# A graph layer on one core: a void block and the odd group at the front, one set of node windows at the end, and a catch-up of five for four

## The chip, the cores and the metric

One core of one Trainium2 chip. The metric is device microseconds for one execution, the median of several runs (three for the kernel before: 2513.2 us, 2512.73 to 2515.78). The engines are PE (TensorE: matmuls and their weight loads), DVE (VectorE), ACT (ScalarE), POOL (GpSimd, which here mostly issues gathers) and SP (which here only issues transfers). They run beside each other, each through its own list of instructions in order, and wait for one another by semaphores.

## What is computed

A graph network layer with a layer norm ahead of it: 6250 nodes of 256 numbers, 206250 edges sorted by destination, 33 per node on average, 64 attributes and one polarity per edge.

```python
h = jnp.maximum(_layernorm(x, axis=-1), 0.0)
polarity = jnp.clip(edge_attr[:, 0:1], 0.0, 1.0)
e = jax.nn.relu(raw @ W_e1.T + b_e1) @ W_e2.T + b_e2
edge_emb = (e * (polarity + 0.01)) @ W_le.T + b_le
msg = jax.nn.relu(h[src] + edge_emb)
aggr = jax.ops.segment_sum(msg, dst, num_segments=h.shape[0])
g = (h + aggr) @ W_g1.T + b_g1
hn = (g - mu) * jax.lax.rsqrt(var + LN_EPS) * ln_g + ln_b
out = x + jax.nn.relu(hn) @ W_g2.T + b_g2
```

All in float32.

## The kernel before

Units, blocks, groups. A tile is 128 edges. A block is four tiles (512 edges), a group is six blocks (GE = 3072 edges). 67 full groups and one odd block of 426 edges make NB = 403 blocks. A unit is half a block, two tiles; there are 806 units. A pair is two blocks that share one load of raw attributes (`load_pair`, L234). In a group the tiles are laid out so that each of the four tiles of a block covers its own run of destinations; `sel` (L589) is a matrix of 128 edges by 32 rows that says which edge adds to which row.

Per pair, `first_layer` (L239) does the first edge layer: eight records of L250 on PE, each block giving two 128x512 results in PSUM that ACT (L259, three of them) and DVE (L256, one) pass through a relu into `e1`. Per unit, `edge_part` (L266) multiplies by the product of the two following weight matrices (four matmuls, eight records, L274) and DVE adds a bias into `msg` (L279); where `plain(u)` holds, in a third of the first units, ACT copies instead (L277) and DVE adds the bias later (L607). `turn_of` (L291) is called at every fourth unit and puts in the next layers, the sums that have become possible and the next loads; in the middle of the run it does two pairs at a time every eighth unit. PSUM has seven banks in one ring for all this (`psz`, L226) and one for the sums.

The other half of a unit is `whole` (L601): DVE multiplies the message by the polarity and adds the gathered row of `hb_d` (L609, two instructions), ACT applies the relu (L614). `hb_d` is the normalized input plus b_le; POOL gathers its rows (L560). The first four units (RAW) are gathered straight from x before `hb_d` exists (L347); their statistics (L457 to L462), normalization (L466) and b_le (L605) are done apart. `add_up` (L616) sums whole units into a group's rows in PSUM (L626), `keep` (L633) copies a finished group to `ms`.

The lead-in (L432 to L459) goes through x in 13 chunks, twelve of four tiles and one of 106 rows: DVE takes statistics (`stats`, L369), ACT a square root (`root`, L376), ACT and POOL make the rows, SP stores them (`nodes_out`, L380). Between the chunks it puts LEAD = 22 units of the edge work. Their `whole` halves must wait for `hb_d`; the main loop (L779 to L801) catches up on them, two whole units for each new one, until they stand a fixed lag behind. That lag is 18 units at first and one at the end.

Nodes are finished in 49 windows of 128 (`node_work`, L674) as soon as the groups that reach into them are summed: `rows_of` (L720) adds the groups' rows to the node (L726), `one`, `two` and `three` are the first matmul (L170) with statistics, the transposition (L186) and the second matmul (L196) with the addition of x (L198) and the store. They are put between units by a list of due units. Two windows are left for the end, since their last group is the last full one or the odd block: window 47 and window 48. Their steps are written out by hand in L802 to L830. In `windows_of` (L64) a group reaches MARGIN = 768 edges beyond its own; a check on the real destinations (`verdict`, L526) sends inputs that exceed this to another way through the data (`any_order`).

The order on each engine is the order in which the program issues the work (`tc.manual_schedule()`).

## Time and profile before

| | us |
|---|---|
| runs of before | 2512.73, 2513.20, 2515.78 (median 2513.2) |
| profiled execution | 2537.35 |
| its span, first to last instruction | 2535.6 |
| mean granted clock of PE in it | 0.967 of full speed |
| busy in the span: PE / DVE / POOL / ACT | 2368.3 / 1657.0 / 1634.3 / 983.4 |
| lead-in and catch-up, as shown below | 0 to 135 |
| from the last edge matmul to the last addition | 2515.46 to 2530.20 |

In the profile, a row of a group has the line, engine, operation, what it writes from what it reads, shapes and count, then busy time and mean duration in ns, then the idle time of the engine just before and who ended it. A row of the timeline has its start, its length, engine, line and operation, the count of instructions merged into it, and in brackets the idle time before it with the one that ended it. "issue" is time in which the engine waited for nothing that the profile shows. Busy time of PE is modelled and instructions overlap, so that starts to starts say more than durations. A float32 matmul shows as two records.

### The profile page before, as it was taken

To read this page: it belongs to the slowest core of one execution; us is meant where nothing else is said; L and a number is where in the kernel's file an instruction comes from. 1 tells how busy PE (TensorE), PEld (TensorE's weight loads), DVE (VectorE), ACT (ScalarE), POOL (GpSimd) and SP (SyncE) were. 2 spreads that over 40 slices of the span, in tenths; PEclk is the share of its full clock that TensorE was granted. 3 is DMA by queue.
4 is the path that set the end of the run, shared out by engine and by line. 5 is a ranking of instruction groups with operands and counts; after the bars stand their busy time and mean duration, and the time that the engine had idled before them with its cause. 6 is when DMAs were issued, how large, how long until landed. Compare 5 with 4: busy or idle time off the path is not lost.

```text
span 2535.6 us, 35656 instructions
## 1 busy us (share of the span) xinstructions
PE 2368.3 (93%) x12382; PEld 1669.2 (66%) x12382; DVE 1657.0 (65%) x3975; ACT 983.4 (39%) x1710; POOL 1634.3 (64%) x1675
## 2 busy tenths in 40 slices
PE   9989999999999999999999999999999999999978
PEld 6666666676766666666766766666766666666646
DVE  7866566666767666665666666666766666666736
ACT  7433333333433433343333333333433333333313
POOL 7666666666666666666666666666666666666661
PEclk9999999999999999999999999999999999999979
DMA  9444344433443443434343444344334334433441
GB/s 308 132 119 121 105 126 119 125 119 106 120 134 115 126 119 102 132 112 127 120 129 112 127 117 120 107 123 121 117 115 128 118 113 118 126 115 109 121 117 41
DMA packets 156226, 309.23 MB, mean 122 GB/s; under 512 B 33327, under 2 KB 78088, under 8 KB 156040
## 3 DMA queue, kind: packets, MB, share of 16 engines
q0 software_dynamic: 77376, 211.39, 28.8%
q1 hardware_dynamic: 77364, 92.23, 11.6%
q10 hardware_dynamic: 1300, 3.28, 0.4%
q8 instruction: 98, 1.61, 0.3%
q14 instruction: 88, 0.72, 0.1%
HBM read 293.92 MB, written 12.85 MB: 121 GB/s over the span
## 4 chain that ended last, share of the span: by engine, by line
PE 86%; issue 6%; DVE 5%; another core or an unknown queue 1%; ACT 1%; DVEq 0%; ACTq 0%
PE pz L274 53%; PE pz L250 17%; PE pd L626 10%; PE pz L726 2%; PE pz L170 2%; PE pz L196 2%; DVE hg L609 2%; DVE msg L279 1%; ACT e L259 1%; PE pz L186 1%; DVE st L141 0%; DVE e L256 0%; DVE sel L589 0%; ACT xt L388 0%
## 5 line engine op out<-in xcount | busy, mean ns | idle before, releaser
L560 POOL DMA_INDIRECT hg<-hb_d,src_s x1604 | 1589.3, 991 | 842.5 <-issue 481.3
L274 PE MATMUL pz<-wc_s,e 128*128 128x256 f32 x6448 | 1484.4, 385 | 34.3 <-issue 26.7
L274 PEld LDWEIGHTS pz<-wc_s,e 128*128 128x128 f32 x6448 | 1220.1, 192 | 303.9 <-issue 95.2
L614 ACT ACTIVATE hg<-hg 128x512 f32<-128x512 f32 x805 | 507.1, 631 | 934.3 <-DVE hg L609 760.2
L279 DVE TENSOR_TENSOR msg<-pz,bc_s 128x512 f32<-128x512 f32 x799 | 547.1, 686 | 233.7 <-remote 86.8
L609 DVE SCALAR_TENSOR_TENSOR hg<-msg,pol_s,hg 128x256 f32<-128x256 f32 x1612 | 697.0, 480 | 0.4
L256 DVE TENSOR_SCALAR e<-pz,vecs 128x512 f32<-128x512 f32 x201 | 150.4, 748 | 568.7 <-PE pz L250 192.3
L250 PE MATMUL pz<-raw,we_s 64*128 64x512 f32 x1612 | 480.2, 661 | 24.3 <-issue 18.3
L259 ACT ACTIVATE e<-pz,vecs 128x512 f32<-128x512 f32 x605 | 376.3, 685 | 318.0 <-remote 112.9
L626 PE MATMUL pd<-hg,sel 128*32 128x256 f32 x3216 | 280.5, 389 | 82.8 <-issue 74.6
L250 PEld LDWEIGHTS pz<-raw,we_s 64*128 64x128 f32 x1612 | 170.5, 198 | 240.9 <-issue 176.4
L626 PEld LDWEIGHTS pd<-hg,sel 128*32 128x32 f32 x3216 | 116.0, 110 | 264.2 <-issue 215.0
L589 DVE SCALAR_TENSOR_TENSOR sel<-iota_w,zero_c,rel 128x128 f32<-128x128 f32 x403 | 138.6, 344 | 0.0
L638 ACT ACTIVATE ms<-pd 128x256 f32<-128x256 f32 x66 | 25.3, 384 | 257.9 <-PE pz L274 92.8
L726 PE MATMUL pz<-s,ms 128*128 128x128 f32 x548 | 74.6, 280 | 6.1 <-issue 5.6
L726 PEld LDWEIGHTS pz<-s,ms 128*128 128x128 f32 x548 | 71.1, 194 | 11.6 <-issue 7.7
L701 DVE SCALAR_TENSOR_TENSOR hT<-hT,zero_c,stb 128x128 f32<-128x128 f32 (+1 forms) x196 | 67.1, 343 | 2.3 <-issue 2.3
L170 PE MATMUL pz<-wg_s,hT 128*128 128x256 f32 (+1 forms) x196 | 51.6, 386 | 7.0 <-DVE hT L728 4.7
L196 PE MATMUL pz<-wg_s,nT 128*128 128x256 f32 (+1 forms) x196 | 51.2, 381 | 1.3 <-issue 0.6
L170 PEld LDWEIGHTS pz<-wg_s,hT 128*128 128x128 f32 (+1 forms) x196 | 36.1, 190 | 16.1 <-DVE hT L728 7.5
L196 PEld LDWEIGHTS pz<-wg_s,nT 128*128 128x128 f32 (+1 forms) x196 | 37.0, 190 | 7.7 <-issue 1.7
L392 POOL TENSOR_TENSOR hb<-xt,rows_b 128x256 f32<-128x256 f32 (+1 forms) x49 | 34.2, 729 | 12.0 <-issue 5.4
(98 smaller groups left out, 415.4 us busy)
## 6 DMA issues: line engine op xcount, KB each, us to landing
raw<-in_raw_t_dram SPq DMA_DIRECT2D x202, 256.0 KB
hg<-hb_d,src_s POOLq DMA_INDIRECT x1604
stb<-st_d SPq DMA_DIRECT2D x49, 128.0 KB
hb_d<-hb SPq DMA_DIRECT2D x12, 512.0 KB
xt<-in_x_dram SPq DMA_DIRECT2D x48, 128.0 KB
hT<-in_x_t_dram SPq DMA_DIRECT2D x48, 128.0 KB
out_dram<-ot SPq DMA_DIRECT2D x48, 128.0 KB
xt<-in_x_dram SPq DMA_DIRECT2D x11, 512.0 KB
```

What stands on the lines that cost most here:

```text
L196: nc.tensor.matmul(po[:n, 0, :], nT[:, c, :n], wg2_s[:, c, :], start=c == 0, stop=c == 1)
L250: z = nc.tensor.matmul(pe[s, c], we1_s[s * F:(s + 1) * F, c * P:(c + 1) * P], raw[q][s * F:(s + 1) * F, :], start=True, stop=True)
L256: nc.vector.tensor_scalar(e1[b][:, c, :], pe[s, c], be1_s[:, c:c + 1], 0.0, op0=ALU.add, op1=ALU.max)
L259: nc.scalar.activation(e1[b][:, c, :], pe[s, c], AF.Relu, bias=be1_s[:, c:c + 1])
L274: last_z = nc.tensor.matmul(pz[:, i, :], e1[b][:, c, k:k + P], wc_s[:, c, :], start=c == 0, stop=c == 1)
L279: nc.vector.tensor_add(msg[u], pz, bc_s)
L560: g = nc.gpsimd.indirect_dma_start(out=hg[u][:, i, :], out_offset=None, in_=hb_d, in_offset=bass.IndirectOffsetOnAxis(ap=src_s[:, 2 * u + ...
L589: nc.vector.scalar_tensor_tensor(sel[g][:, k * S:(k + 1) * S, :], iota_w.rearrange("p (o w) -> p o w", o=1).to_broadcast([P, S, W]), zero_ ...
L609: nc.vector.scalar_tensor_tensor(hg[u][:, i, :], m[:, i, :], pol_s[:, 2 * u + i:2 * u + i + 1], hg[u][:, i, :], op0=ALU.mult, op1=ALU.add)
L614: nc.scalar.activation(hg[u], hg[u], AF.Relu)
L626: z = nc.tensor.matmul(acc[g][j * W:(j + 1) * W, :], sel[g][:, k * S + j, :], m[:, j % 2, :], start=k == 0, stop=b == blocks_of(g)[-1])
L726: nc.tensor.matmul(pa[:, c, :n], ms[g][:, c * P:(c + 1) * P], box["sel2"][i][:, :n], start=i == 0, stop=i == len(gs) - 1)
```

## The change

The odd group moves to the front: block 0 is void and never computed, block 1 is group 0 (512 edges), groups 1 to 67 are full and the last one carries the padding. There are still 403 blocks with work and 806 units, now numbered 2 to 807 (U0 = 2). The first raw tile has one block in it, so the first layer has half its matmuls; the first call of `turn_of` comes at unit 2. All that ran at a unit's number in the main loop is shifted by U0, except the turns, which stay on multiples of four and eight.

In the catch-up five whole units are made for every four new ones instead of two for one. In the lead-in the last full chunk of x and the chunk of 106 rows are both stored one step earlier, with the statistics of the short one ahead; the statistics of the four raw units take their scratch from pool `w0` instead of `p1`. At the end only window 48 is left, because the last group reaches back by LAST = 512 edges; its sums of the earlier group and the bias of its first matmul are put ahead of the last whole units, the last group is copied in halves by ACT and DVE, and what is due of other windows comes between its steps. `dst` and the check on destinations follow the new layout.

```diff
@@ -31,11 +31,14 @@
 NF = E // GE
-NB = NF * L + 1
+NB = NF * L + 2
 NT = NB * S
...
 MARGIN = 768
+SP = S * P
+LAST = 512
+U0 = 2
 DEG = E // N
...
@@ -54,17 +57,18 @@
 def group_of(b):
-    return b // L
+    return (b + L - 2) // L
 
...
 def blocks_of(g):
-    return range(g * L, min((g + 1) * L, NB))
+    return range(max(1, 2 + (g - 1) * L), 2 + g * L)
 
...
 
-    lo = (GE * g - MARGIN) // DEG
-    hi = (GE * (g + 1) + MARGIN) // DEG
+    a, b = (SP + GE * (g - 1), SP + GE * g)
+    lo = (a - (LAST if g == NG - 1 else MARGIN)) // DEG
+    hi = (b + MARGIN) // DEG
     return [w for w in range(NW) if w * P <= hi and (w + 1) * P > lo]
...
@@ -162,14 +166,17 @@
 
-        def first(aT, bias_by_pe=False):
+        def bias():
             ph = ps()
-            if bias_by_pe:
-                nc.tensor.matmul(ph[:n, 0, :], ones[0:1, :n], bg1_b[0:1], start=True, stop=False)
+            nc.tensor.matmul(ph[:n, 0, :], ones[0:1, :n], bg1_b[0:1], start=True, stop=False)
+            return ph
+
+        def first(aT, begun=None):
+            ph = ps() if begun is None else begun
             for c in range(2):
-                nc.tensor.matmul(ph[:n, 0, :], aT[:, c, :n], wg1_s[:, c, :], start=c == 0 and not bias_by_pe, stop=c == 1)
+                nc.tensor.matmul(ph[:n, 0, :], aT[:, c, :n], wg1_s[:, c, :], start=c == 0 and begun is None, stop=c == 1)
             hs = nd.tile([P, D], F32, name="hs")
-            if bias_by_pe:
+            if begun is not None:
                 hb = ph[:, 0, :]
...
@@ -177,7 +184,8 @@
             one_over_std(rs[:n], mv, n)
-            nc.vector.tensor_scalar(hs[:n], hb[:n], mv[:n, 0, 0:1], rs[:n], op0=ALU.subtract, op1=ALU.mult)
+            for h in ([slice(0, P), slice(P, D)] if begun is not None else [slice(0, D)]):
+                nc.vector.tensor_scalar(hs[:n, h], hb[:n, h], mv[:n, 0, 0:1], rs[:n], op0=ALU.subtract, op1=ALU.mult)
             return hs
...
@@ -238,20 +246,20 @@
 
-            bs = [b for b in (2 * q, 2 * q + 1) if b < NB]
+            bs = [b for b in (2 * q, 2 * q + 1) if 1 <= b < NB]
             if not bs:
...
             for c in range(2):
-                for s, b in enumerate(bs):
+                for s, b in ((b % 2, b) for b in bs):
                     pe[s, c] = ps().rearrange("p a b -> p (a b)")
...
             for c in range(2):
-                for s, b in enumerate(bs):
+                for s, b in ((b % 2, b) for b in bs):
                     if s == c == 1:
...
@@ -261,7 +269,7 @@
 
-            return u < LEAD and u % 3 == 1
+            return u < U0 + LEAD and u % 3 == 1
 
...
@@ -306,7 +314,7 @@
             edge_part(u)
-            if u % 4 == TURN:
+            if u % 4 == TURN or u == U0:
                 turn_of(u // 4)
...
@@ -326,7 +334,7 @@
-        nc.scalar.dma_start(out=src_0, in_=src_c[:, :2 * RAW])
+        nc.scalar.dma_start(out=src_0, in_=src_c[:, 2 * U0:2 * U0 + 2 * RAW])
...
@@ -430,17 +437,23 @@
             for k in range(len(parts) + 1):
-                if k < len(parts):
+                last = len(parts) - 1
+                if k < last - 1:
                     stats(k, 0, 2)
+                if k == last:
+                    stats(k, 0, CH)
+                    root(k)
                 if k == 0:
...
                     product()
-                if k:
+                if 0 < k <= last:
                     nodes_out(k - 1)
                     load_rows(k - 1 + AHEAD)
-                if k < len(parts):
-                    stats(k, 2, CH)
+                if k == last:
+                    nodes_out(k)
+                if k < last:
+                    stats(k, 2 if k < last - 1 else 0, CH)
                     root(k)
...
@@ -455,7 +468,7 @@
                 for m in range(n * RAW // 2, (n + 1) * RAW // 2):
-                    row_stats(p1, P, 2, lambda i: hg[m][:, i, :], mv_0[:, 2 * m:2 * m + 2, :])
+                    row_stats(w0, P, 2, lambda i: hg[U0 + m][:, i, :], mv_0[:, 2 * m:2 * m + 2, :])
                 forward(u)
...
@@ -479,17 +492,17 @@
-            nc.tensor.matmul(pb[:, :NF, :], ones[0:1, :],
-                             dst_f[0:1, :full].rearrange("o (g r) -> o g r", r=L * S)[:, :, :S], start=True, stop=True)
-            nc.tensor.matmul(pb[:, NF, :], ones[0:1, :], dst_f[0:1, full:], start=True, stop=True)
+            nc.tensor.matmul(pb[:, 1:, :], ones[0:1, :],
+                             dst_f[0:1, 2 * S:].rearrange("o (g r) -> o g r", r=L * S)[:, :, :S], start=True, stop=True)
+            nc.tensor.matmul(pb[:, 0, :], ones[0:1, :], dst_f[0:1, S:2 * S], start=True, stop=True)
...
-                rel[:, :full].rearrange("p (g k j) -> p g k j", k=L, j=S),
-                dst_f[:, :full].rearrange("p (g k j) -> p g k j", k=L, j=S),
-                base_b[:, :NF, :].rearrange("p g (o j) -> p g o j", o=1).to_broadcast([P, NF, L, S]), ALU.subtract)
-            nc.vector.tensor_tensor(rel[:, full:], dst_f[:, full:], base_b[:, NF, :], ALU.subtract)
+                rel[:, 2 * S:].rearrange("p (g k j) -> p g k j", k=L, j=S),
+                dst_f[:, 2 * S:].rearrange("p (g k j) -> p g k j", k=L, j=S),
+                base_b[:, 1:, :].rearrange("p g (o j) -> p g o j", o=1).to_broadcast([P, NF, L, S]), ALU.subtract)
+            nc.vector.tensor_tensor(rel[:, S:2 * S], dst_f[:, S:2 * S], base_b[:, 0, :], ALU.subtract)
...
@@ -573,7 +587,7 @@
                 spent += us
-                while (got - 2 * RAW) * STEP < spent + AFLOAT and got < 2 * min(NU, 4 * summed + HG):
+                while (got - 2 * (U0 + RAW)) * STEP < spent + AFLOAT and got < 2 * min(NU, max(U0, 4 * summed) + HG):
                     gather(behind)
...
@@ -583,7 +597,7 @@
 
-                t = (g * L + k) * S
+                t = blocks_of(g)[k] * S
                 if k == 0:
...
@@ -616,9 +630,9 @@
-                k = b - g * L
+                k = b - blocks_of(g)[0]
...
-                    acc[g] = pd[:, g % 2, :] if g < NG - 1 else ps()[:, 0, :]
+                    acc[g] = pd[:, g % 2, :]
...
@@ -634,10 +648,12 @@
                     ms[g] = ms_p.tile([P, D], F32, name="ms")
-                    if g != NG - 2:
-                        nc.scalar.activation(ms[g], acc.pop(g), AF.Copy)
+                    a = acc.pop(g)
+                    if g < NG - 1:
+                        nc.scalar.activation(ms[g], a, AF.Copy)
                     else:
-                        nc.vector.tensor_copy(ms[g], acc.pop(g))
+                        nc.scalar.activation(ms[g][:, :P], a[:, :P], AF.Copy)
+                        nc.vector.tensor_copy(ms[g][:, P:], a[:, P:])
                     sel.pop(g)
...
@@ -651,9 +667,9 @@
                     for b in (2 * summed, 2 * summed + 1):
-                        if b < NB:
+                        if 1 <= b < NB:
                             whole_groups.append(add_up(b))
-                            if b % L == 0 and group_of(b) + 2 < NG:
+                            if b == blocks_of(group_of(b))[0] and group_of(b) + 2 < NG:
                                 rest.extend(select(group_of(b) + 2))
...
@@ -710,6 +726,10 @@
 
+                def begin():
+                    sums_of(gs[:-1])
+                    box["ph"] = bias()
+
                 def halves_out():
...
@@ -727,17 +747,17 @@
                                                    op1=ALU.add)
-                    if gs[-1] < NG - 2:
+                    if gs[-1] < NG - 1:
                         at(now + far_apart[0], one)
...
                 def one():
-                    box["hs"] = first(box["hT"], gs[-1] >= NG - 2)
-                    if gs[-1] < NG - 2:
+                    box["hs"] = first(box["hT"], box.get("ph"))
+                    if gs[-1] < NG - 1:
                         at(now + far_apart[1], two)
...
                     box["nT"] = second(box["hs"])
-                    if gs[-1] < NG - 2:
+                    if gs[-1] < NG - 1:
                         at(now + far_apart[2], three)
...
@@ -747,9 +767,9 @@
                     at(now + 2, spread)
-                if gs[-1] < NG - 2:
-                    return lambda: at(now + 2, rows_of)
-                ending[gs[-1] - NG].append((sums_of, halves_out, rows_of, one, two, three, gs))
+                if gs[-1] < NG - 1:
+                    return lambda: at(now + 2 - (gs[-1] == NG - 2), rows_of)
+                ending.append((begin, sums_of, halves_out, one, two, three, gs))
                 return lambda: None
...
@@ -771,12 +791,12 @@
                           (8, node_weights)):
-                at(LEAD + i, fn)
+                at(U0 + LEAD + i, fn)
             for i, fn in enumerate((by_group(0, ALU.max), by_group(1, ALU.min), by_row(0, ALU.max), by_row(1, ALU.min),
                                     verdict, count, total)):
-                at(LEAD + 22 + 5 * i, fn)
+                at(U0 + LEAD + 22 + 5 * i, fn)
             flag = None
-            for u in range(LEAD, NU):
+            for u in range(U0 + LEAD, NU):
                 now = u
...
@@ -784,8 +804,8 @@
                 piece()
-                lag = max(LEAST, LEAD - RAW - u // SHRINK) + (by_two(u // 4) and (u + 1) % 8 == TURN)
-                ready_for = min(u + 1 - lag, 2 * (u + 1 - LEAD))
+                lag = max(LEAST, LEAD - RAW - (u - U0) // SHRINK) + (by_two(u // 4) and (u + 1) % 8 == TURN)
+                ready_for = min(u + 1 - lag, U0 + 5 * (u + 1 - U0 - LEAD) // 4)
                 while made < ready_for:
...
@@ -797,35 +817,25 @@
                             late[w] = node_work(w, True)
-                if u == LEAD + 60:
+                if u == U0 + LEAD + 60:
                     flag = nc.values_load(bad_i[0:1, 0:1], min_val=0, max_val=3 * P)
+            while steps:
+                steps.popleft()[1]()
+            for begin, sums_of, halves_out, one, two, three, gs in ending:
+                begin()
+            while made < NU:
+                whole(made)
+                made += 1
+            add_pairs(last=True)
+            for begin, sums_of, halves_out, one, two, three, gs in ending:
+                sums_of(gs[-1:])
+                halves_out()
+                one()
             while todo:
...
                     fn()
-            while steps:
-                steps.popleft()[1]()
-            before, last = ending[-2], ending[-1]
-            for sums_of, halves_out, rows_of, one, two, three, gs in before:
-                rows_of()
-            for sums_of, halves_out, rows_of, one, two, three, gs in last:
-                sums_of(gs[:-1])
-            while made < NU:
-                whole(made)
-                made += 1
-            for sums_of, halves_out, rows_of, one, two, three, gs in before:
-                one()
-            add_pairs(last=True)
-            for sums_of, halves_out, rows_of, one, two, three, gs in last:
-                sums_of(gs[-1:])
-                halves_out()
-            for sums_of, halves_out, rows_of, one, two, three, gs in before:
-                two()
-            for sums_of, halves_out, rows_of, one, two, three, gs in last:
-                one()
-            for sums_of, halves_out, rows_of, one, two, three, gs in before:
-                three()
-            for sums_of, halves_out, rows_of, one, two, three, gs in last:
+            for begin, sums_of, halves_out, one, two, three, gs in ending:
                 two()
...
@@ -954,12 +964,11 @@
 
-        a = padded(a, NT * P, fill)
-        a = a.reshape((NT, P) + a.shape[1:])
-        o = np.empty_like(a)
-        n = NF * L * S
-        o[:n] = np.swapaxes(a[:n].reshape((NF, S, L) + a.shape[1:]), 1, 2).reshape(o[:n].shape)
-        o[n:] = a[n:]
+        a = padded(a, (NT - S) * P, fill)
+        a = a.reshape((NT - S, P) + a.shape[1:])
+        o = np.full((NT, P) + a.shape[2:], fill, a.dtype)
+        o[S:2 * S] = a[:S]
+        o[2 * S:] = np.swapaxes(a[S:].reshape((NF, S, L) + a.shape[1:]), 1, 2).reshape(o[2 * S:].shape)
         return o
```

36 lines of the change are left out of this document (18 added, 18 removed).

## The prediction

> **What bounds the kernel now.** I read the page first (shares, the chain of waits, the costliest groups), then windows of a few microseconds, then the timeline of the first 135 us and of the last 30.
>
> ```profile
> PE 2368.3 (93%) x12382; PEld 1669.2 (66%) x12382; DVE 1657.0 (65%) x3975; ACT 983.4 (39%) x1710; POOL 1634.3 (64%) x1675
> ...
> PE 86%; issue 6%; DVE 5%; another core or an unknown queue 1%; ACT 1%; DVEq 0%; ACTq 0%
> ...
> L274 PE MATMUL pz<-wc_s,e 128*128 128x256 f32 x6448 | 1484.4, 385 | 34.3 <-issue 26.7
> ...
> L614 ACT ACTIVATE hg<-hg 128x512 f32<-128x512 f32 x805 | 507.1, 631 | 934.3 <-DVE hg L609 760.2
> ...
> L250 PE MATMUL pz<-raw,we_s 64*128 64x512 f32 x1612 | 480.2, 661 | 24.3 <-issue 18.3
> ...
> L626 PE MATMUL pd<-hg,sel 128*32 128x256 f32 x3216 | 280.5, 389 | 82.8 <-issue 74.6
> ```
>
> PE (TensorE) carries 86% of the chain. Nearly all of that is per unit of edges (L274), per pair of blocks (L250) and per summed block (L626), and the change leaves those counts alone: 806 units and 403 blocks before and after (the void block has no matmul). So only the places where PE waits can pay: the start, where VectorE (DVE) is behind, and the end.
>
> ```profile
> 76.93:80.74 3.81, 0.00 (x1) 0.03 (x1) 3.77 (x8) 1.26 (x2) 3.23 (x2) 1.00 0.23 70
> 82.60:89.90 7.30, 6.80 (x17) 3.26 (x15) 6.17 (x15) 5.35 (x9) 5.19 (x5) 0.55 0.35 97
> 2440.00:2470.00 30.00, 15.87 (x34) 8.98 (x34) 0.61 (x2) 1.66 (x4) 19.35 (x21) 0.51 0.33 95
> ```
>
> In these windows the columns are length, busy time of PE, its weight load, DVE, ACT, POOL, granted clock, DMA share and GB/s. PE stands still for 3.81 us while DVE is busy for 3.77, and then runs 7.3 us at 0.55 of its clock. The last row is a stretch in which PE crawls with nobody to wait for. It explains most of why the profiled execution (2537.35 us, span 2535.6, so 1.75 around it) is 24.2 us over the median 2513.2. I work out differences in the profiled execution and apply them to the median; this stretch is no part of the edit.
>
> **The change part by part: the lead-in.** The order of the changed kernel's instructions shows PE doing one unit, not two, ahead of the layer of the third raw tile.
>
> ```profile
> 14.14 3.62 PE L274 MATMUL pz<-wc_s,e 128*128 128x256 f32 x16
> 18.69 1.99 PE L250 MATMUL pz<-raw,we_s 64*128 64x512 f32 x8 [0.93 <-DMA raw<-in_raw_t_dram]
> ...
> 17.58 0.69 DVE L279 TENSOR_TENSOR msg<-pz,bc_s 128x512 f32<-128x512 f32 x1 [1.95 <-ACT xt L388]
> ...
> 21.00 0.72 DVE L256 TENSOR_SCALAR e<-pz,vecs 128x512 f32<-128x512 f32 x1
> ```
>
> That layer waits for its DMA until 18.69, and the loads ahead of it on SP's queue are the same. So the second unit falls behind it. Unit cost: 64 records of L274 take 14.01 us (row below), eight units, 1.75 each. DVE gets the layer's fourth relu straight after the first message, so it sits from about 18.2 to 20.65 in front of five statistics blocks that used to fill that time; 2.4 us late there; how much of that is made up before 65 I leave to the bounds. I take PE's 1.75; bounds 0 and 2.8 (the whole of 15.9 to 18.69). The first unit of the main loop then starts at 66.88 + 1.75 = 68.6 (66.88 is the end of the L250 that begins below at 64.96 and takes 1.92).
>
> ```profile
> 60.50 0.42 DVE L141 BATCH_NORM_STATS2 st<-hg 128x6 f32<-128x256 f32 x1
> ...
> 61.05 0.40 DVE L141 BATCH_NORM_STATS2 st<-hg 128x6 f32<-128x256 f32 x1
> ...
> 64.96 1.99 PE L250 MATMUL pz<-raw,we_s 64*128 64x512 f32 x8
> ...
> 66.93 0.98 POOL L560 DMA_INDIRECT hg<-hb_d,src_s  x1 [3.34 <-DVE msg L279]
> ...
> 68.57 0.99 DVE L468 TENSOR_SCALAR pol_s<-pol_s 128x1612 f32<-128x1612 f32 x1
> 68.69 4.04 ACT L466 ACTIVATE hg<-hg,nm,rs 128x256 f32<-128x256 f32 x8 [0.47 <-DVE nm L462]
> ...
> 71.83 0.88 DVE L609 SCALAR_TENSOR_TENSOR hg<-msg,pol_s,hg 128x256 f32<-128x256 f32 x2
> 72.62 0.69 DVE L605 TENSOR_TENSOR hg<-hg,rows_b 128x512 f32<-128x512 f32 x1
> 73.23 0.69 DVE L607 TENSOR_TENSOR msg<-msg,bc_s 128x512 f32<-128x512 f32 x1
> 73.95 0.88 DVE L609 SCALAR_TENSOR_TENSOR hg<-msg,pol_s,hg 128x256 f32<-128x256 f32 x2
> ...
> 78.38 1.83 DVE L488 TENSOR_TENSOR rel<-dst_f,base_b 128x1608 f32<-128x1608 f32 x1
> 80.51 0.69 DVE L279 TENSOR_TENSOR msg<-pz,bc_s 128x512 f32<-128x512 f32 x1
> 81.11 0.34 DVE L589 SCALAR_TENSOR_TENSOR sel<-iota_w,zero_c,rel 128x128 f32<-128x128 f32 x1
> 81.38 0.68 DVE L607 TENSOR_TENSOR msg<-msg,bc_s 128x512 f32<-128x512 f32 x1
> 94.24 1.13 DVE L506 TENSOR_SCALAR rowid<-base_b,p 32x68 f32<-32x68 f32 x4
> ```
>
> Starts to starts give DVE's prices: message 0.60, whole unit 0.79, b_le 0.61, the bc addition 0.71, sel 0.27, rel 1.87 (with its short second half), polarity twice 0.99, row numbers 1.15, one statistics block 0.55 (60.50 to 61.05, two instructions), relu of a layer at most 0.72.
>
> **The catch-up.** Before, DVE makes two whole units for each unit of PE from the first, and the first sums stand at the fourth; PE waits for their sel (3.81), then for messages. In the changed kernel the eight statistics blocks of the raw rows come after the relu of the layer at 65.1 (68.6 less two units), one sum step of five blocks comes at unit 33 instead of one of two and one of four, and units 24 and 25 are followed by two layers at once. DVE's list from 65.1 to the whole of unit 11, which the last of those sums needs: 3 relus 2.1, statistics 4.4, the root of their variances 0.4 (an estimate, two short operations), polarity 2.0, 9 messages 5.4, 10 wholes 7.9, 4 b_le 2.4, 3 bc 2.1, rel 1.9, 5 sel 1.35, row numbers 1.15: 31.1, ending at 96.2; with ACT's relu (631 ns in its group) that is 96.8.
>
> PE meanwhile: two units to 72.1, four layer matmuls to 74.0. The next four need banks: the third of them the message of unit 25 (75.8 in DVE's list) and the fourth ACT's first relu, which stands behind eight normalizations (4.04 us from 70.7) and the relu of a whole unit, so until 76.5. PE resumes with unit 26 at about 77.1. Eight units 14.0 and the small matmuls 0.7 end at 91.8, a layer at 93.7, three of the five blocks' sums at 95.2; the rest waits to 96.8 and ends at 97.3. The next layer waits for the message of unit 33 (98.8: two messages, a whole and two sel after 96.2) and ends at 99.8. Eight units, layer, four blocks, layer (14.0 + 1.92 + 2.0 + 1.92) bring unit 42 to 119.6. DVE's list in that time is 19 us, so it no longer decides.
>
> ```profile
> 109.09 14.01 PE pz L274 x64
> 123.10 1.92 PE pz L250 x8
> ...
> 135.09 4.95 PE pz L274 x22
> ```
>
> Before, unit 42 starts at 135.09. There 764 units are left, in the changed kernel 766, half a layer more (0.96) and one block's sum (0.5): 3.5 + 1.0 + 0.5 = 5.0. From 123.10 to 135.09 the rows of before hold 12.0 us for work worth 1.92 + 2.0 + 1.92; the other 6.1 are issue waits after a burst of small matmuls, which I charge to both. The head gains 135.09 - 6.1 - 119.6 - 5.0 = 4.4. Lower bound: the catch-up saves nothing and the lead-in's 2.8 stay (-2.8); upper bound: the 6.1 go too (+10.5).
>
> By the rows, each wait of PE in that sketch is under 2 us. With a dip of the clock like the one above it would lose 7.3 x 0.45 = 3.3. [...]
>
> Edits at nothing: the scratch from another pool and the order of the last two chunks let the first gather go earlier, which stood 3.34 us for DVE at 66.93. No PE work waits for it: whole units read gathered rows only from the fifth on, about 81 in my list. If that cover is gone it is worth at most those 3.34, not counted.
>
> **The end.**
>
> ```profile
> 2515.39 1.93 PE L626 MATMUL pd<-hg,sel 128*32 128x256 f32 x32
> 2515.50 0.69 DVE L279 TENSOR_TENSOR msg<-pz,bc_s 128x512 f32<-128x512 f32 x1
> 2517.25 1.92 PE L726 MATMUL pz<-s,ms 128*128 128x128 f32 x12
> ...
> 2520.60 1.13 PE L170 MATMUL pz<-wg_s,hT 128*128 128x256 f32 x4
> 2521.66 0.64 PE L626 MATMUL pz<-hg,sel 128*32 128x256 f32 x8
> ...
> 2523.07 0.69 PE L710 MATMUL pz<-s,ms 128*128 128x106 f32 x4 [0.77 <-ACT ms L638]
> 2523.58 0.49 DVE L717 SCALAR_TENSOR_TENSOR hT<-hT,pz 128x106 f32<-128x106 f32 x2
> 2525.77 0.43 DVE L141 BATCH_NORM_STATS2 st<-pz 106x6 f32<-106x256 f32 x1 [1.70 <-PE pz L170]
> 2529.78 0.42 DVE L198 TENSOR_TENSOR ot<-pz,xt 106x256 f32<-106x256 f32 x1 [1.93 <-PE pz L196]
> ```
>
> From PE's last edge unit (2515.46) to the end of the last addition (2530.20) are 14.74. In the changed kernel the chain is: 0.3 of DVE backlog, the message 0.60, two wholes 1.58 and their relu 0.6 (3.1); last sums 0.25 and half a copy each on ACT and DVE 0.35 (3.7, estimates); L710's two matmuls and the two halves 1.0 (4.7); the second half of L170 0.6 (5.3); from the statistics to the end 4.43 as before, less 0.1 for the split (9.6). That saves 5.1. But window 47's work moves ahead of that point, onto a busy PE: 12 records of L726 (1.7, the 1.92 of the row less the short wait for ms inside it), L170 1.07, and three blocks' sums, 24 of the 32 records in 2.0 (1.5): 4.3. Net 0.8; bounds -1.5 (a DVE backlog of a whole unit and message more, and window 47's matmuls late) and +3 (part of the 4.3 falls into waits PE has anyway).
>
> Sum: 4.4 + 0.8 = 5.2 us off; 2537.35 would be 2532.1, and the median 2508.0.
>
> **The rivals.**
>
> 1. Little is left: a half clock returns once (-3.3) and the end brings nothing (-0.8), so 1.1 remain: 2512.1. For it: DVE is busy at every moment from 65 to 98 in my list, so any slip reaches PE. Against: PE needs only the last two of five blocks' sums late.
>
> 2. Slower. Mechanism: DVE does not clear its backlog, because the statistics (4.4) now stand behind the relu at 65.1. Then PE waits at the sums of units 33, 41 and 49, each wait long enough for a half clock. Price: 2 us and 3.3 each, three times, 16, against a head of 4.4 and an end of 0.8: 10.7 over, and 5.4 over with two of the three; 2518.6 to 2523.9. It decides from the point where unit 11's whole is later than about 101, four us past my list. For it: the row 76.93 shows this very wait. Against: DVE's share over the span is 65%, and the 19 us list between units 34 and 42 fits.
>
> 3. The issue waits after the first bursts (6.1) go with the smaller backlog: 2508.0 - 6.1 = 2501.9. For it: they follow the burst in which DVE had just caught up. Against: 74.6 us of issue idle before L626's matmuls in the whole run.
>
> **How the numbers follow.** Forecast 0.48, rival 1 0.25, rival 2 0.15, rival 3 0.12. About 0.2% (5.0 us) is what a measurement of this kernel can tell from no change. The forecast lies just beyond it, and its own range, 2502 to 2512 from the smaller unknowns, lies more on the faster side than not, since the upper bounds of both terms are wider than the lower; I count 0.36 of its chance as faster and 0.12 as same. Rival 1 is the same, rival 3 faster, rival 2 slower but for 0.02. Faster 0.36 + 0.12 = 0.48, same 0.12 + 0.25 + 0.02 = 0.39, slower 0.13. The range reaches down to 2500 for rival 3 and up to 2518.5 for the start of rival 2.
>
> **What would show it.** Unit 2 done by 16 and the next L274 only after 20.6; DVE in front of a relu at 18 to 20. No PE pause over 3 us between 66 and 120, and no 0.5 clock there; a short PE wait at sums near 95. Unit 42 between 119 and 126. At the end one set of statistics, about 9.6 us from the last edge matmul to the last addition. Wrong, if PE pauses over 3 us again before its sums, if DVE is still full after 125, or if the end is longer than 12.

## The result and the profile after

Side by side on one chip, 22 runs each, the changed kernel took 2521.97 us (median; 2513.17 to 2530.76) and the kernel before 2514.57: ratio 1.0025, interval 1.0013 to 1.0036. By the ratio that is 6.3 us slower (the two medians stand 7.4 apart), where 5.2 faster was forecast. In the later sets the kernel before took 2181 us in two and 2554 to 2557 in three, one chip giving both at different hours, so only ratios inside a set are compared. The unchanged text of the changed kernel, over all sets:

```
set of runs          before, us   ratio changed / before   interval
first                2514.6       1.0025                   1.0013 to 1.0036
a2_changed_again     2180.6       0.9998                   0.9989 to 1.0007
a3_changed_third     2556.7       1.0000                   0.9975 to 1.0024
a4_changed_fourth    2555.0       1.0007                   0.9990 to 1.0024
a5_changed_fifth     2555.0       0.9973                   0.9956 to 0.9990
```

The last two are the same text beside the same runs of before and stand 0.34% apart, so the intervals are too narrow for what one kernel does from one load to the next. The first set's 0.25% was not seen again; the five ratios average 1.0001. What has to be explained is less a loss than why neither term of the forecast gain arrived.

The page of the changed kernel (first profile, 2529.66 us, span 2527.9), engines and the chain:

```profile
PE 2364.1 (94%) x12376; PEld 1666.4 (66%) x12376; DVE 1655.9 (66%) x3978; ACT 983.0 (39%) x1710; POOL 1636.8 (65%) x1675
...
PE 85%; issue 6%; DVE 5%; another core or an unknown queue 2%; DMA 1%; ACT 1%; SPq 0%; DVEq 0%; ACTq 0%
```

Nearly the shares of before, with DMA new in the chain. Its timeline of PE, and three windows of it (columns as in the prediction):

```profile
13.86 1.89 PE L282 MATMUL pz<-wc_s,e 128*128 128x256 f32 x8
20.07 3.78 PE L258 MATMUL pz<-raw,we_s 64*128 64x512 f32 x8 [4.32 <-DMA raw<-in_raw_t_dram]
...
75.48 3.70 PE L258 MATMUL pz<-raw,we_s 64*128 64x512 f32 x12
80.20 2.69 PE L258 MATMUL pz<-raw,we_s 64*128 64x512 f32 x4 [1.01 <-DVE msg L287]
82.82 3.78 PE L282 MATMUL pz<-wc_s,e 128*128 128x256 f32 x8
...
102.00 1.98 PE L258 MATMUL pz<-raw,we_s 64*128 64x512 f32 x6
...
105.29 2.81 PE L640 MATMUL pd<-hg,sel 128*32 128x256 f32 x40
...
114.31 14.41 PE L282 MATMUL pz<-wc_s,e 128*128 128x256 f32 x64
```
```profile
20.00:24.00 4.00, 3.93 (x9) 1.39 (x10) 0.07 (x1) 1.38 (x3) 0.00 (x0) 0.50 1.09 351
...
80.20:88.00 7.80, 7.80 (x17) 4.52 (x17) 4.19 (x8) 4.10 (x8) 5.73 (x6) 0.54 0.34 101
...
105.30:114.30 9.00, 7.33 (x49) 2.86 (x48) 4.62 (x11) 4.63 (x9) 5.96 (x6) 0.85 0.74 240
```

PE stands for 4.32 us ahead of the third raw tile's layer and comes back at half clock (0.50 from 20.00 to 24.00). The two layers after unit 25 need 7.3 us (75.48 to 82.82) where 3.8 is their work, and from within the second of them PE is at half clock (0.54 over the 7.8 us from 80.20), with no pause over 1.01. The layer behind the first sums takes until 114.31.

From here on, units of edges are counted in the order in which PE makes them, from 0. Number 22 is the first of the main loop in both kernels, and number 40 in the changed kernel is the prediction's "unit 42". It starts at 134.35, against 119.6 forecast without issue waits, 125.7 with the 6.1 of them that were charged to both. The 8.7 split so: 3.3 to number 22 (71.94 for 68.6); 2.4 from there to number 24 (10.9 for 8.5); 4.5 over the eight units from number 24 to 102.00 (19.2 for 14.7); and 1.5 less after that (32.4 for 33.9).

The end, from the last units on:

```profile
2507.96 3.72 PE L282 MATMUL pz<-wc_s,e 128*128 128x256 f32 x16
...
2514.51 0.71 ACT L626 ACTIVATE hg<-hg 128x256 f32<-128x256 f32 x2
...
2515.93 0.28 ACT L655 ACTIVATE ms<-pd 128x128 f32<-128x128 f32 x1 [0.71 <-PE pd L640]
2516.24 0.29 DVE L656 COPY ms<-pd 128x128 f32<-128x128 f32 x1 [2.26 <-ACT ms L655]
...
2518.24 0.43 DVE L145 BATCH_NORM_STATS2 st<-pz 106x6 f32<-106x256 f32 x1 [0.88 <-PE pz L177]
...
2522.23 0.42 DVE L206 TENSOR_TENSOR ot<-pz,xt 106x256 f32<-106x256 f32 x1 [1.72 <-PE pz L204]
```

From the last edge matmul (2511.68) to the last addition (2522.65) are 10.97, not 9.6. Counted from that matmul, the last relu ends at 3.5 (forecast 3.1), both copies at 4.85 (3.7), and the statistics start at 6.6 (5.3). DVE's copy waits for ACT's (it starts 0.31 behind it), and ACT's for the last sums.

### The profile page after: what moved, and what is told of

The parts are those of the page before. It is cut to its first block, busy times and chain, and to the rows that moved or that the text cites. A ratio compares the mean times of both kernels' runs of the same rounds, so it can differ in the third digit from the quotient of the medians.

```text
span 2527.9 us, 35635 instructions
## 1 busy us (share of the span) xinstructions
PE 2364.1 (94%) x12376; PEld 1666.4 (66%) x12376; DVE 1655.9 (66%) x3978; ACT 983.0 (39%) x1710; POOL 1636.8 (65%) x1675
## 4 chain that ended last, share of the span: by engine, by line
PE 85%; issue 6%; DVE 5%; another core or an unknown queue 2%; DMA 1%; ACT 1%; SPq 0%; DVEq 0%; ACTq 0%
PE pz L282 53%; PE pz L258 17%; PE pd L640 9%; PE pz L746 2%; PE pz L177 2%; DVE hg L623 2%; PE pz L204 2%; DVE msg L287 1%; DMA raw<-in_raw_t_dram 1%; ACT e L267 0%; PE pz L194 0%; DVE sel L603 0%; DVE e L264 0%; DMA hT<-in_x_t_dram 0%
## 5 line engine op out<-in xcount | busy, mean ns | idle before, releaser
L258 PE MATMUL pz<-raw,we_s 64*128 64x512 f32 x1612 | 487.0, 655 | 33.6 <-issue 19.5
L640 PE MATMUL pd<-hg,sel 128*32 128x256 f32 x3224 | 261.4, 391 | 65.2 <-issue 59.8
L746 PEld LDWEIGHTS pz<-s,ms 128*128 128x128 f32 x548 | 69.8, 192 | 7.6 <-issue 4.1
L177 PE MATMUL pz<-wg_s,hT 128*128 128x256 f32 (+1 forms) x196 | 52.6, 391 | 10.3 <-DVE hT L748 7.8
```

The source lines that it names most:

```text
L177: nc.tensor.matmul(ph[:n, 0, :], aT[:, c, :n], wg1_s[:, c, :], start=c == 0 and begun is None, stop=c == 1)
L258: z = nc.tensor.matmul(pe[s, c], we1_s[s * F:(s + 1) * F, c * P:(c + 1) * P], raw[q][s * F:(s + 1) * F, :], start=True, stop=True)
L640: z = nc.tensor.matmul(acc[g][j * W:(j + 1) * W, :], sel[g][:, k * S + j, :], m[:, j % 2, :], start=k == 0, stop=b == blocks_of(g)[-1])
L746: nc.tensor.matmul(pa[:, c, :n], ms[g][:, c * P:(c + 1) * P], box["sel2"][i][:, :n], start=i == 0, stop=i == len(gs) - 1)
```

## The experiments

Theories: A, the lead-in; B, the catch-up; C, DVE's list at units 22 to 25; later G, the gathers, and P, chance of the clock. Each variant was timed beside the kernel before; a label starting with e, g or t is a variant, a2 to a5 are the unchanged text of the changed kernel, b2 that of the kernel before.

**The lead-in.** In `forward`, e1 puts the layer of the third raw tile after the second unit; e5 does the same and has the early statistics of e4 below as well.

```diff
-            if u % 4 == TURN or u == U0:
+            if u % 4 == TURN or u == U0 + 1:
```

> The changed kernel, but the layer of the third raw tile comes after the second unit again, as before the change. Theory A (the lead-in loses it: PE stood idle for 4.32 us before that layer and then ran at 0.50 of its clock): the pause shrinks to about 2.6, no window at 0.5 around 20 to 26, the first unit of the main loop 4 to 5 us earlier than in the changed kernel, and the time 4 to 5 us below the changed kernel's, so 1 to 3 over before. Theory B (the catch-up loses it): the lead-in's gain is swallowed by the waits at 76 to 92, so the time stays within 1 us of the changed kernel's.

> Statistics early, and the layer of the third raw tile after the second unit. Theory A adds its part: 2 to 5 us under the kernel with early statistics alone. Theory C alone: within 1 us of it, since what the early landing gives is lost by waiting for DVE or the transfers later in the lead-in.

Measured: e1 1.0025 (1.0001 to 1.0049), e5 1.0018 (1.0009 to 1.0027), the latter 5.5 us over e4b by the medians of one set. The pause at the third tile went and came back two tiles later, at the fifth (4.76 us in e5, 1.91 in e1). PE and SP's queue of e5, then SP's queue of the changed kernel (a2):

```profile
37.58 3.79 PE L258 MATMUL pz<-raw,we_s 64*128 64x512 f32 x8 [4.76 <-DMA raw<-in_raw_t_dram]
...
29.45 1.88 SPq L245 DMA_DIRECT2D raw<-in_raw_t_dram  x1
```
```profile
23.86 1.36 SPq L245 DMA_DIRECT2D raw<-in_raw_t_dram  x1
25.32 0.39 SPq L401 DMA_DIRECT2D hb_d<-hb  x1
25.81 2.76 SPq L374 DMA_DIRECT2D xt<-in_x_dram  x1
```

The turn that makes the layer also asks for the raw tile two pairs on. Called one unit later, that load falls behind a store and a chunk of x on SP's queue, 29.45 for 23.86. Theory A's remedy falls: putting the layer early is what keeps the fifth tile in time.

**The catch-up.**

```diff
 # e2, in the changed kernel
-                ready_for = min(u + 1 - lag, U0 + 5 * (u + 1 - U0 - LEAD) // 4)
+                ready_for = min(u + 1 - lag, U0 + 2 * (u + 1 - U0 - LEAD))
 # e3, in the kernel before
-                ready_for = min(u + 1 - lag, 2 * (u + 1 - LEAD))
+                ready_for = min(u + 1 - lag, 5 * (u + 1 - LEAD) // 4)
```

> The changed kernel with the old catch-up, two whole units for each new one. By the prediction the slower catch-up saves the wait for sel and a half clock, 3 to 7 us, so this kernel would be that much slower than the changed one. Theory B (five for four brings nothing or harms): within 1 us of the changed kernel, or up to 4 faster, since the first sums stand earlier and their work is spread over more turns. The lead-in, untouched, should show the same 4.3 us pause at 16 to 20 in either case.

> The kernel before with five whole units for four new ones and nothing else of the change. By the prediction (the wait of 3.81 us for sel and the 7.3 us at 0.55 go): 3 to 7 us faster than before. Theory B: within 1 us of before, or slower, with a wait and a window at half clock at another place of 75 to 130.

Measured: e2 1.0002 (0.9984 to 1.0020), e3 0.9998 (0.9983 to 1.0013). The catch-up alone, either way, moves nothing that can be measured; in e3 the wait for sel went, and PE waited 0.43 and 1.52 for messages in the next layer instead.

**The statistics of the raw rows** (theory C). In the changed kernel they come with the last two units of the lead-in; e4 and its repeat e4b put them two units earlier, e6 and e8 do so with other catch-ups.

```diff
+                if k == len(parts):
+                    for m in range(RAW):
+                        row_stats(w0, P, 2, lambda i: hg[U0 + m][:, i, :], mv_0[:, 2 * m:2 * m + 2, :])
                 for _ in range((k > 0) + (k > 2 and k % 3 > 0)):
 ...
             for n, u in enumerate(units):
-                for m in range(n * RAW // 2, (n + 1) * RAW // 2):
-                    row_stats(w0, P, 2, lambda i: hg[U0 + m][:, i, :], mv_0[:, 2 * m:2 * m + 2, :])
                 forward(u)
 # e6: U0 + 2 * (u + 1 - U0 - LEAD); e8: U0 + 3 * (u + 1 - U0 - LEAD) // 2
```

> The changed kernel with the statistics of the four raw units two units earlier, ahead of the last layer of the lead-in. Theory C (DVE's list after that layer's relu, with 5.2 us of statistics in it, holds the message and the relus that the two layers at 75 to 82 wait for): the waits there shrink from about 1.8 us to under 0.5, the half clock of 80.9 to 91 goes, and the time is 3 to 6 us below the changed kernel's. Rival: the layers wait for ACT's normalizations and the statistics only take idle time of DVE either way; within 1 us of the changed kernel.

> The changed kernel once more, for a second profile and for a time on the chip of the three others. Theory A (the layer after one unit always costs a pause over 3.4 us and a half clock): pause of about 4 us at 16 to 20 again and the main loop's first layer pair at 75. Rival: the landing of the third raw tile differs from run to run, and the pause is under 2 us here. Theory C (statistics in front of the messages): the wait between units 23 and 24 is again 2 to 4 us over the 5.6 that one unit and two layers take, and the clock falls behind it.

> The changed kernel with the statistics two units earlier, beside the changed kernel on one chip. Theory C: 4 to 8 us faster than the changed kernel, no wait over 0.5 us between units 23 and 24. Rival (its better ratio was chance): within 2 us of the changed kernel.

> Statistics early, and two whole units for each new one. If the catch-up matters by itself, the wait for messages between units 23 and 26 comes back here and the time is 2 to 4 us over the kernel with early statistics alone; if it only mattered through DVE's backlog, within 1 us of it.

> The kernel before once more, for a second profile of it. If the waits called issue after the sums at 126 to 132 and in the rest of the run belong to the kernel, they are here too, with the same clock; if they belong to the chip, they go or move with the time of the whole run. The wait for sel at 77 to 81 and the half clock behind it belong to the kernel and should be here in any case, 3 to 4 us and one or two windows.

> Statistics early, and three whole units for two new ones, between the changed and the old catch-up. Theory (five for four leaves 3 us of waiting for messages at the third sums near 135 to 145, two for one 3 us at units 23 to 26): this one loses under 1.5 at either place and is 1 to 4 us faster than before. Rival: what is saved at one sum step is waited for at another, within 1 us of before.

Measured: e4 0.9994 (0.9971 to 1.0017), e4b 0.9997 (0.9988 to 1.0006), e6 0.9997 (0.9988 to 1.0006), e8 1.0003 (0.9994 to 1.0012). In the two sets at 2181 us PE has next to no issue waits (issue is 0% of a2's chain), so the start can be read without them. Starts of units, from the timelines:

```
unit number             22     24     46      48      90      790      span
before (b2)             66.27  70.78  132.17  135.63  252.79  2119.81  2178.2
changed (a2)            67.38  78.09  136.41  145.65  256.30  2123.26  2181.9
statistics early (e4b)  67.62  75.27  129.68  142.02  253.33  2120.29  2179.0
```

PE of b2 and one window of it; then the same of a2:

```profile
80.13 0.64 PE L626 MATMUL pd<-hg,sel 128*32 128x256 f32 x8 [3.81 <-DVE sel L589]
...
76.50:86.70 10.20, 6.29 (x29) 2.63 (x30) 9.95 (x22) 5.27 (x10) 8.28 (x7) 0.83 0.30 83
```
```profile
70.92 3.70 PE L258 MATMUL pz<-raw,we_s 64*128 64x512 f32 x12
75.63 2.54 PE L258 MATMUL pz<-raw,we_s 64*128 64x512 f32 x4 [1.01 <-DVE msg L287]
78.09 3.78 PE L282 MATMUL pz<-wc_s,e 128*128 128x256 f32 x8
...
68.00:76.50 8.50, 7.49 (x29) 4.17 (x28) 7.94 (x17) 5.84 (x12) 6.67 (x7) 1.00 0.40 121
76.50:86.70 10.20, 10.20 (x23) 6.64 (x22) 5.00 (x9) 4.15 (x8) 4.94 (x6) 0.50 0.27 82
```

Before pays 3.81 us for sel and then a mean clock of 0.83 over 10.2 us: 1.7 us. Changed takes 7.2 us for 3.84 of work in its two layers (a3, at full clock there, 6.4, so that about 2.6 are waits) and then has all of the 10.2 us at 0.50: 5.1. Its longest single pause there is 1.01. In e4b, PE and then DVE:

```profile
71.17 4.17 PE L258 MATMUL pz<-raw,we_s 64*128 64x512 f32 x16
75.27 1.99 PE L282 MATMUL pz<-wc_s,e 128*128 128x256 f32 x8
...
137.47 1.12 PE L258 MATMUL pz<-raw,we_s 64*128 64x512 f32 x2 [0.39 <-DVE msg L287]
139.12 2.96 PE L258 MATMUL pz<-raw,we_s 64*128 64x512 f32 x6 [0.53 <-DVE msg L287]
```
```profile
130.19 0.48 DVE L624 SCALAR_TENSOR_TENSOR hg<-msg,pol_s,hg 128x256 f32<-128x256 f32 x1 [0.71 <-DMA hg<-hb_d,src_s]
...
134.53 0.48 DVE L624 SCALAR_TENSOR_TENSOR hg<-msg,pol_s,hg 128x256 f32<-128x256 f32 x1 [0.97 <-DMA hg<-hb_d,src_s]
134.93 1.82 DVE L530 TENSOR_REDUCE far<-dst_f 128x67 f32<-128x1608 f32 x1
...
136.73 0.68 DVE L287 TENSOR_TENSOR msg<-pz,bc_s 128x512 f32<-128x512 f32 x1
```

The layers take 4.1 and the half clock is gone (1.00 from 71.00 to 86.70): theory C holds for that place. By unit 46 e4b is 6.7 us ahead of a2. Then it needs 12.3 us for the two units with the third sums where a2 needs 9.2: DVE has caught up with the gathers and waits for them, then makes 1.8 us of the check on destinations (L530), and PE waits for the message behind both. In a2 the same check starts at 138.97 and its message, at 140.77, is in time, since PE is later there. Which of the two costs more in e4b no run separates. 3.0 of the 6.7 are left at unit 90, 0.5 short of before. The time is before's. So C is right about the wait and wrong about the total. In e6 the wait of C comes back (number 24 follows number 22 by 9.2 us, for 7.7 in e4b), with no half clock behind it, and the time is the same.

**The gathers** (theory G). In b2 and e4b they run one behind another, 62 by 150 us; a2 made 59, after one gap:

```profile
87.19 0.94 POOL L574 DMA_INDIRECT hg<-hb_d,src_s  x1 [4.10 <-PE pz L282]
```

They are held in step with PE's work, so PE at half clock holds them too; the theory was that their lateness is met at the next sums. g1, g2 and g3 let them go further ahead.

```diff
-AFLOAT = 6.0
+AFLOAT = 14.0
```

> The changed kernel a third time, beside the three below. Theory G (the gathers set the head: they run one behind another from about 66 on, and in both profiles of this kernel they stood once for 4 us at 82 to 92 for a matmul of PE, since they are held in step with PE's work): the gap of about 4 us is here again, and the kernel is about as far behind its gathers as behind before's time. Rival: the gap was a matter of the lead-in's pause and is absent when the third raw tile lands in time.

> The changed kernel with the gathers allowed 14 us of work ahead of PE instead of 6 (AFLOAT). Theory G: no gap over 1 us in the gathers between 67 and 110 on account of PE, three gathers more by 150 than in the changed kernel, and 2 to 4 us off its time in runs without other loss. Theory C alone (statistics and messages): the gap goes, but PE's waits at 71 to 80 and the half clock behind them stay, and the time with them, within 1 us.

> Gathers 14 us ahead and the statistics early. Theory G: since early statistics had left no gap in the gathers, nothing more to win: within 1 us of the kernel with early statistics alone, 0 to 2 us under before. Rival (DVE bound): 3 us or more under the kernel with gathers ahead alone.

> The kernel before with the gathers 14 us ahead, as a control. On a quick chip its gathers had no gap in the head, so theory G expects nothing: within 1 us of before, whichever chip this is but for gaps that chip itself puts between gathers.

Measured: a3 1.0000, g1 1.0003 (0.9981 to 1.0026), g2 1.0011 (0.9983 to 1.0039), g3 1.0002 (0.9979 to 1.0024), in a set at 2557 us with issue waits. a3 has neither the 4 us gap nor the half clock at 76 to 87; a5, with one step of 3.41 us of it, has a gap of 1.8:

```profile
76.50:86.70 10.20, 10.20 (x45) 8.01 (x44) 8.90 (x17) 5.77 (x11) 8.07 (x8) 1.00 0.36 104
...
97.00:106.30 9.30, 7.40 (x44) 2.60 (x36) 4.09 (x10) 4.23 (x8) 6.06 (x7) 0.80 0.70 225
```

So the gap goes with the half clock and not with the gathers' own pace, and G as stated falls; gathers ahead win nothing that can be measured. What stays shown is the smaller claim, that DVE in e4b waited for gathers where PE came early.

**The end and the edits at nothing.** t1 puts windows 47 and 48 both at the end; e9 restores the order of the last two chunks of x and the pool of the scratch.

```diff
 # t1
-LAST = 512
+LAST = 768
 # e9
-                    row_stats(w0, P, 2, lambda i: hg[U0 + m][:, i, :], mv_0[:, 2 * m:2 * m + 2, :])
+                    row_stats(p1, P, 2, lambda i: hg[U0 + m][:, i, :], mv_0[:, 2 * m:2 * m + 2, :])
-                if k == last:
-                    stats(k, 0, CH)
-                    root(k)
...
-                if k == last:
-                    nodes_out(k)
```

> The changed kernel with LAST = 768, so that windows 47 and 48 both end with the last group and two sets of node work stand at the end, as before the change. By the prediction's sum (5.1 off the end, 4.3 of it back onto a busy PE) it is 0.8 us slower than the changed kernel, from last edge matmul to last addition 3 to 5 us longer and the time up to the last edge matmul 3 to 4 us shorter. Rival (the moved work falls into waits): 2 to 4 us slower.

> The changed kernel with the last two chunks of x in the old order and the scratch of the raw statistics from pool p1 again. By the prediction (edits at nothing): within 1 us of the changed kernel, with the first gather of the main loop 2 to 4 us later and no longer waits of PE. Rival: the gathers land late for DVE's first whole units, and units 23 to 30 come 2 to 4 us later.

e9: 1.0006 (0.9997 to 1.0015), not to be told from a2's 0.9998; the forecast of within 1 us is finer than these intervals. Its first gather is at 72.1 for 67.2 in a2, 2.4 of it from its own later unit 22 (69.8), and no unit is later for it (unit 90 at 255.6 for 256.3). But its statistics show what the pool does. Two blocks in a2's order of work (first profile of the changed kernel), then two of e9:

```profile
73.25 0.43 DVE L145 BATCH_NORM_STATS2 st<-hg 128x6 f32<-128x256 f32 x1
73.72 0.18 DVE L146 BATCH_NORM_AGGREGATE mv<-st 128x2 f32<-128x6 f32 x1
73.93 0.43 DVE L145 BATCH_NORM_STATS2 st<-hg 128x6 f32<-128x256 f32 x1
...
74.50 0.66 DVE L287 TENSOR_TENSOR msg<-pz,bc_s 128x512 f32<-128x512 f32 x1
```
```profile
67.02 0.42 DVE L145 BATCH_NORM_STATS2 st<-hg 128x6 f32<-128x256 f32 x1
67.47 0.18 DVE L146 BATCH_NORM_AGGREGATE mv<-st 128x2 f32<-128x6 f32 x1
67.57 0.40 DVE L145 BATCH_NORM_STATS2 st<-hg 128x6 f32<-128x256 f32 x1
```

0.68 from block to block in pool w0, which has one buffer, so that a block begins when the second operation of the last has ended (73.90); 0.55 in p1, which has four. Over eight blocks that is 1.0 us of DVE, and number 24 follows number 22 by 8.9 us in e9 for 10.0 in a3 and a4, the profiles of the changed kernel without a half clock there.

t1: 1.0057 (1.0043 to 1.0071), but not for the reason on record. PE and SP's queue of t1:

```profile
2131.82 3.78 PE L258 MATMUL pz<-raw,we_s 64*128 64x512 f32 x8 [3.95 <-DMA raw<-in_raw_t_dram]
...
2124.35 0.77 SPq L214 DMA_DIRECT2D xt<-in_x_dram  x2
...
2126.47 0.92 SPq L245 DMA_DIRECT2D raw<-in_raw_t_dram  x2
```

The loads of two windows stand ahead of a raw tile on SP's queue, PE stands 3.95 us and its clock falls: the eight records behind the pause take 3.78 us, the same eight at 2145.56 take 1.99. Behind the last edge matmul its span has 22.7 us for a2's 16.4, 6.3 more where 3 to 5 were forecast, with half clock from 2178.79 on. That isn't the end that the kernel before has, so the size of the end's term is read from the profiles instead: from the start of unit 790 to the end of the span 58.3 and 58.4 in the two of before, 58.5, 58.6, 58.5, 58.5 and 58.6 in the five of the changed kernel.

**Chance of the clock** (theory P).

> The changed kernel a fourth time. Theory P (chance of the clock: the waits of about 2 us between units 23 and 25 are always there, but they halve the clock for 10.2 us only where they fall into one of the clock's steps of 3.41 us): its runs fall into two groups 3 to 5 us apart on a quick chip, the profile shows the half clock near 76 to 91 where its own time is in the slower group and none where it is in the faster, and the median stays within 0.1% of before. Rival (the kernel is slower by 0.25%, as on the first chip): median 5 to 6 us over before.

> The same once more, for a second profile and twice the runs: theory P and its rival as for the run beside it.

a4 and a5 ran in a set near 2555 us, where two groups 3 to 5 us apart don't stand out, so P's test by times is not decided. a4 has no half clock at 76 to 87 (1.00) and its own run (2558.57) is above its median, a5 has one step of it (0.83 over the 10.2 us) and is above its median too; a3, without one, is the quickest of its set. a2's runs do fall apart, seven at 2178.3 to 2180.6 and four at 2182.7 to 2185.4, the profiled one (2183.67) among the four; but e4b, whose profile has no half clock there, spreads nearly as widely (2176.9 to 2183.6), so this counts for little.

The five profiles say more: two have half clock there for 10.2 us, one for 3.4 and two none, with the same pause of 1.01 in the same place each time. Within one trace the falls of the clock lie whole steps of 3.41 us apart (first profile: 19.45, 80.89 and 111.61, 18 and 9 steps; a5: 77.55, 104.85 and 166.29, 8 and 18), so the steps can be laid back over the pause. One step of a2, then two of a3:

```profile
73.06:76.47 3.41, 2.40 (x7) 0.80 (x6) 3.13 (x6) 3.38 (x7) 2.59 (x3) 1.00 0.35 96
```
```profile
71.92:75.33 3.41, 3.06 (x12) 0.94 (x8) 3.34 (x7) 3.41 (x7) 2.80 (x3) 1.00 0.24 73
75.33:78.74 3.41, 2.75 (x9) 1.55 (x10) 2.22 (x5) 3.37 (x6) 2.50 (x4) 1.00 0.36 109
```

In a2 the whole pause lies in one step, and the clock falls where that step ends. The first profile (77.48 to 80.89) and a5 (74.14 to 77.55) have the same 2.40 of 3.41 and the same fall. In a3 a step ends inside the pause and the clock stays; a4 is alike (3.09 and 2.72). So in these five profiles the same pause cost a half clock or not by where the steps lay, as P says. What a step must hold is not settled: in e6 one with only 2.32 busy (74.29 to 77.70) was followed by no fall. Nor is it why the half clock lasted three steps twice and one in a5, with PE busy throughout.

## Why the prediction was wrong

**The step that failed is the head's 4.4.** Three of its terms did.

*Waits under 2 us were taken to leave the clock alone.* In a2 no pause between units 22 and 24 is longer than 1.01, and 10.2 us run at 0.50. A dip like that of before was priced at 3.3 and left out of the 4.4, so the 4.4 rests on waits under 2 us costing no clock. That was the author's assumption, and no run shows it: the same pause of 1.01 had 10.2 us at 0.50 behind it in a2 and none in a3 and a4. Nor did PE stand for a whole step: in a2 it was busy for 2.40 of the 3.41 us that ended with the fall at 76.47. The stretches at 0.50 measured here are 3.4 us (b2), 6.8 (first profile of before) and 10.2 (a2): one, two and three of the 3.41 us steps between falls.

*What before loses was read from one execution.* Its 7.3 us at 0.55 were counted as a loss that the change removes. In b2 the dip is 3.4 long (6.8 in the first profile) and number 42 starts at 125.16, 3.8 earlier than in the first profile without its 6.1 of issue waits. b2 ran in the set at 2181 us, so that part of the 3.8 may belong to that condition; as far as it belongs to the kernel, most of the 4.4 lay there.

*The list for units 22 to 25 was 1.5 short.* Number 24 follows number 22 by 10.0 us in a3 and a4, not 8.5 (10.3 to 10.9 in the other three, with half clock in it). The statistics are the cause (early, it is 7.7): the message that frees the second layer's bank stands behind all eight, and they take 5.3 and not 4.4. The e9 rows show where that 0.9 comes from; it is one of the edits at nothing, the scratch: the prediction asked what its new place frees and not how many buffers the place has.

*A term that was wrong without making the miss.* Half a layer was priced at 0.96. A layer with one block in it took as long as one with two (1.98 and 1.99 us). The odd block's layer of b2, then a full one of a2:

```profile
2138.66 1.98 PE L250 MATMUL pz<-raw,we_s 64*128 64x512 f32 x4
```
```profile
2139.03 1.99 PE L258 MATMUL pz<-raw,we_s 64*128 64x512 f32 x8
```

The next instructions start 1.91 and 1.92 later; in a full layer the records of the two blocks start 0.01 us apart and run beside each other. Without the 0.96 the forecast of the head would have been 5.4, further off.

**What held, in part.** The lead-in's 1.75, bounds 0 to 2.8: number 22 stands at 67.4 to 68.0 in the four later profiles, before's at 66.3 to 66.9. But the pause ahead of the third tile's layer was no accident of the first profile (4.32, number 22 at 71.9): e6, e8 and e9, with the same instructions up to there, show 2.21, 3.77 and 3.09, and number 22 at 68.8 to 70.3. The issue waits charged to both: in a3 the layer behind the first sums takes from 99.31 to 106.35, 5.1 more than its work (the last part of it at half clock, from 102.64 on). In the sets at 2181 us both kernels have next to none, and the work that took 12.0 in the first profile of before takes 5.7 in b2 (119.46 to 125.16). Not all of the 6.1 was waiting: from 130.07 to 133.48 that profile is at half clock. With neither the pause nor the half clock at 76, a3's number 40 starts at 127.6 for the 125.7 of the forecast. The order of the chunks and the earlier first gather were worth nothing that can be measured.

**The end** was forecast at 0.8 gained, and from unit 790 on it is about 0.2 longer. That stretch holds one block's sums more than before (96 records for 88, 0.5 us), which the prediction had counted in the head; by its own books the end gained about 0.3. The size of the work moved ahead was right (4.2 for 4.3: from unit 790 to the last edge matmul 42.3 us in a2, 38.1 in b2); the relu and the half copies after the last edge matmul were the greater part of what was 1.4 too small (10.97 for 9.6).

**Where the gain went.** One sure wait of 3.81 for sel became about 2.6 us of shorter ones in two layers, with a chance of 5.1 us at half clock behind them; and of the time that e4b won before unit 46, part was waited for at the third sums. Rival 2 had named these sums among its places, and a price of 2 and 3.3 us for each. Its point, the tenth whole unit later than about 101, was passed in the first profile, where the last half of this row is the tenth:

```profile
105.08 1.67 DVE L623 SCALAR_TENSOR_TENSOR hg<-msg,pol_s,hg 128x256 f32<-128x256 f32 x4
```

It was passed in a2 too (102.2), but not in a3 and a4 (97.9). It was passed because PE itself was late, and what PE waited for were banks for its layers; no wait at the first sums reached 3 us. Rival 1, which let one half clock return and the end bring nothing, is nearest to the mean of the five ratios. That the first set was 0.25% slower is not explained by the runs: its profile shows 3.3 us lost by number 40 (134.35 for 135.09 less 4.0, the prediction's 5.0 without the half layer), but the same kernel was level or faster in four later comparisons.

No variant here beats the kernel before by more than its interval. a5 does (0.9973), but it is the changed kernel itself, whose other four sets are level or slower.

## What to carry to other kernels

A saving in the first hundred microseconds is only worth what is left of it several sums later: follow the unit starts to the point where the next producer is met (here the gathers and a check on DVE). A wait of 1 us that may be followed by 10.2 us at half clock (1.01 in a2) is not a small cost, so ask of each wait what clock follows it, and take what the old kernel loses from more than one execution. Before moving a step, list the loads it issues: here the edits that moved one (e1 and e5, t1) put a raw tile behind other loads on the same queue, and PE stood 1.91, 4.76 and 3.95 us.

## What the runs showed of the hardware that was not expected

The same program took 2181 us in two sets and 2515 to 2557 in four, one chip (by its number) being in both kinds. At 2181 us the chain has no issue waits:

```profile
PE 98%; DVE 2%; issue 0%; ACT 0%; DVEq 0%; ACTq 0%
```

That row is a2's; the first profile of the same text has 6% there. Over the whole span PE's issue waits are 1.5 us in a2 and 112 in the first profile, and the granted clock was 0.996 and 0.966. The issue waits seen after bursts of sums, on which a rival was built, thus belong to the machine's condition and not to the kernel. What they are, no run here shows.
